# Placing side jobs' stages by the clock of their first engine in a four-layer gated cross-attention kernel

## The chip, the cores and the metric

The kernel runs on one core of a Trainium2 chip. The metric is the device time of one execution in microseconds (us). Engines are named as in the profile: PE (TensorE matmul), PEld (its weight loads), DVE (VectorE), ACT (ScalarE), POOL (GpSimd), SP (SyncE, which here only issues DMAs). Names such as L222 are lines of the kernel before the change.

## The reference, cut to what matters

Sixteen sequences of 128 tokens with 256 features (`x`), a context of the same shape, and four layers. Each layer adds a gated cross-attention and a gated feed-forward part to `x`:

```python
for l in range(4):
    x = x + tanh(g_xattn[l]) * xattn[l](layernorm(x), ctx)
    x = x + tanh(g_ffn[l]) * ffn[l](layernorm(x))
```

The attentions of layers 0 to 2 have 16 heads of 16 features; layer 1 takes its softmax over the queries and layer 2 has a mask on keys. Layer 3 has 8 heads of 64 features, and its keys and values come from the normalized context together with the normalized `x`. The feed-forward parts of layers 0, 2 and 3 are mixtures of 8 experts of which each token uses the best two; layer 2 has a shared expert besides. Layer 1 is a linear layer with a gated low-rank addition (LoRA). Everything is float32.

```python
probs, idx = top_k(softmax(h @ w_gate.T), 2)
y = sum(probs[j] * expert[idx[j]](h) for j in range(2))
```

## The kernel before, in words

**Tiling.** A sequence is one tile of 128 tokens; four sequences make a block, so there are 16 sequences in 4 blocks. `xs[b]` stays in SBUF throughout. PSUM has eight banks in two pools of four: `ps_mm` (attention scores, experts' hidden values) and `ps_x` (all else). Code that doesn't assume small score ranges (`layers(fast=False)`) is there for other inputs and is not run here.

**Attention.** `attend` runs an attention as a software pipeline over sequences. Step n does `scores` of sequence n (values projection `ps_v`, 16 score matmuls into the four `ps_mm` banks, four exps on ACT), `values` of sequence n-1 (`ps_o`, in layers 0 and 2 with row sums by a matmul and a reciprocal on DVE), and `output` of sequence n-2 (`ps_y`, then the addition to `x` on DVE, L348). Layers 1 and 2 run in one call, as 32 steps.

**Side jobs.** What else the attention needs is written as Python generators, one per block: `queries` (layer norm, transposes, projection, L1165 on), `keys`, the routing of a block that is done (`Moe.front`), and for layer 1 `Lora.run`. A layer norm takes statistics on DVE, `ve` on DVE (L217 or L219), a logarithm and an exponential on ACT (L222, L224), three DVE operations (L227 to L230), and four activations per block on ACT (L306). `front` computes the router's logits, a softmax, the best two experts, the place of every row, and scatters the rows to `xg` in DRAM with eight indirect DMAs on POOL (L529). After some blocks `plan` (L598 on) works out on DVE which expert each slot of 128 rows belongs to; SP reads its result into registers. A generator yields where another engine's result is needed. `yield Pe(...)` says that the next stage begins with matmuls; a plain number says that it doesn't; zero says that it may start at once.

**What sets the order.** PE, ACT and DVE execute in the order in which Python issues instructions (`manual_schedule`, L1483); the other queues, SP and POOL among them, are ordered by the framework. `Clock` (L1311) is a model of the engines' times: `note` adds up each issued instruction's estimated cost and keeps when each tile is written and read. `now()` is PE's time in it. `run_stage` runs one stage of a job and notes the time at which its results are ready. `poll` runs stages that aren't `Pe` as long as any is ready by `now()`; `whole` polls and then runs one ready `Pe` stage; `idle` does the same or moves the PE clock on; `tick` spends up to `share` us of PE time on such work between the parts of a step; `tick.until(tiles)` idles until tiles are ready. The model's waits of an instruction are for its inputs, its engine and the tiles that it overwrites by name, not for a PSUM bank that is used anew under another name.

**Layer 0's early experts.** Once block 1 is routed, a plan gives nine slots that are surely full. `start` (L2352) makes a generator for them, and runs its first stage at once: it issues the loads of rows (L759) and weights (L1533) on SP. `early` (L2356) is the filler: `attend` takes it up when all scores are issued, and interleaves its stages with the routing of blocks 2 and 3. The other 30 slots follow after `attend`. In layers 1 and 2 the filler is the shared expert, in layer 3 the slots (`open_end`).

Of the kernel before, what the change touches and what calls it, by code (L numbers as in the profile page):

```python
# [90 lines left out]
def kernel(ctx: ExitStack, tc: tile.TileContext, a: dict, out: bass.AP):  # L91
    nc = tc.nc
# [4 lines left out]
    rpool = ctx.enter_context(tc.tile_pool(name="route", bufs=2))  # L97
    xtpool = ctx.enter_context(tc.tile_pool(name="xnT", bufs=NBLK))
    dram = ctx.enter_context(tc.tile_pool(name="rows", bufs=1, space=DRAM))
    ps_mm = ctx.enter_context(tc.tile_pool(name="ps_mm", bufs=4, space=PSUM))  # L100
    ps_x = ctx.enter_context(tc.tile_pool(name="ps_x", bufs=4, space=PSUM))

# [96 lines left out]
    class Pe(int):  # L199
        pass  # L200

    def finish(job):

        while True:
            try:
                next(job)
            except StopIteration as end:
                return end.value


    def inverse_sd(var, n, twice):

        ve = stat.tile([P, n], F32, tag="ve", name="ve")
        if twice:
            nc.vector.tensor_scalar(ve, var, 1.0 + 1e-5, 1e-10, ALU.mult, ALU.add)  # L217
        else:
            nc.vector.tensor_scalar(ve, var, 1e-5, None, ALU.add)  # L219

        lv = stat.tile([P, n], F32, tag="sd", name="lv")
        nc.scalar.activation(lv, ve, AF.Ln)  # L222
        r0 = stat.tile([P, n], F32, tag="r0", name="r0")
        nc.scalar.activation(r0, lv, AF.Exp, scale=-0.5)  # L224
# [71 lines left out]
    def normalized(srcs, mv, rstd):  # L296

        nmr = stat.tile([P, len(srcs)], F32, tag="nmr", name="nmr")
        nc.vector.scalar_tensor_tensor(nmr, mv[:, :, 0], -1.0, rstd, ALU.mult, ALU.mult)  # L299
        yield 1  # L300
        while len(held) > 2 and held[-3] is not None:
            yield 1
        xns = stat.tile([P, len(srcs), ROW], F32, tag="xn", name="xn", bufs=3)
        held.append(xns)
        for i, src in enumerate(srcs):
            nc.scalar.activation(  # L306
                xns[:, i, 0:D], src, AF.Identity, bias=nmr[:, i:i + 1], scale=rstd[:, i:i + 1]
            )
            if i == 1:
                yield 1  # L310
        return xns
# [48 lines left out]
    def softmax8(lg):  # L360
# [3 lines left out]
        nc.vector.tensor_tensor(d, lg, bc(m), ALU.subtract)  # L364
        yield 1
        e = small("sm_e")
# [55 lines left out]
    class Moe:  # L422
# [14 lines left out]
        def front(self, blk, plan=None, bias=None):  # L437
# [8 lines left out]
            next(soft)  # L446
            yield 1
            next(soft)
            if self.layer == 2:
                yield 2  # L450
# [654 lines left out]
    class Fast16:  # L1105
# [86 lines left out]
        def scores(self, b, tick):  # L1192
# [17 lines left out]
            else:  # L1210
                nc.vector.tensor_copy(v, pv)

# [96 lines left out]
    }  # L1309

    class Clock:  # L1311

# [18 lines left out]
        def cost(self, ins, out, srcs):  # L1331
# [16 lines left out]
            if ins.engine == mybir.EngineType.Activation:  # L1348
                return 0.13 + n * 0.7e-3 + (0.04 if len(srcs) > 2 else 0.0)
            if ins.engine == mybir.EngineType.Pool:  # L1350
                return 0.1 + n * 2.6e-3
            if kind == "InstReciprocal":
                return 0.1 + n * 6.5e-3
            return 0.07 + n * 0.97e-3

# [21 lines left out]
        def when(self, *tiles):  # L1377
            return max(self.done.get(t.tensor.name, 0.0) for t in tiles)

    def attend(parts, filler=None, open_end=False, hurry=True, share=2.5):  # L1380

# [5 lines left out]

        clock = Clock()
        jobs, filling, waiting = [], [], []

# [3 lines left out]
        def run_stage(job):  # L1394
            clock.ends, clock.moved = [], []
            try:
# [8 lines left out]
                return  # L1405
            job[2] = isinstance(n, Pe)
            ends = clock.ends or clock.moved
# [5 lines left out]
        def poll():  # L1413
            while True:
                for job in list(jobs):
                    if not job[2] and job[1] <= now():
                        run_stage(job)
                        break
                else:
                    return  # L1420

        def whole():
            poll()
            for job in jobs:
                if job[2] and job[1] <= now() + 0.1:
                    run_stage(job)
                    return True
            return False

        def idle(limit):  # L1430


            if whole():
                return
            times = [job[1] for job in jobs] + [limit]
            if filling and min(times) > now() + 0.3:
                if filling[0][1] <= now() + 0.1:
# [5 lines left out]
        class Tick:  # L1443
# [12 lines left out]
            def urgent(self):  # L1456
                for job in jobs:
                    if job[3] and job[2] and job[1] <= now() + 0.1:
                        run_stage(job)
                        self.urgent()  # L1460
                        return
# [7 lines left out]

        def begin(gen, pe, key=False):  # L1470
            return [gen, max(now(), clock.at[mybir.EngineType.DVE]) if not pe else 0.0, pe, key]

        def ahead(att, before, blk):
            made = att.prepare(blk, before(blk) if before is not None else None)
            made = [begin(job, False) for job in made]
            jobs.extend(made)
# [6 lines left out]
        with tc.manual_schedule(engines=IN_ORDER):  # L1483
            ln_exp()
            prepared = ahead(*blocks[0][:2], 0)
            for n in range(len(steps) + 2):
                tick.left = share
                if n == len(steps) - 1 and open_end:
                    next(filler)
                if n == len(steps) and filler is not None:  # L1490
                    filling.append(begin(filler, True))
                if n < len(steps):
# [7 lines left out]
                    tick()  # L1500
                    att, b = steps[n]
                    att.scores(b, tick)
                if 1 <= n <= len(steps):
                    tick.urgent()
                    att, b = steps[n - 1]
                    att.values(b, tick)
                if n >= 2:
                    att, b = steps[n - 2]
                    att.output(b, tick)
                    if b % BPB == BPB - 1:  # L1510
                        _, _, behind, blk = blocks[(n - 2) // BPB]
                        job = begin(behind(blk), False, hurry)
                        waiting.append(job)
# [736 lines left out]
    def layers(fast):  # L2250
# [40 lines left out]
        with tc.tile_pool(name="context", bufs=1) as cpool, ExitStack() as for_mid:  # L2291
# [16 lines left out]
            with tc.tile_pool(name="att0", bufs=2) as pool:  # L2308
# [43 lines left out]
                def start(plan):  # L2352
                    started.append(slots0(moe, n, [plan], lanes, tiles(fpool, bufs0)))
                    next(started[0])

                def early():  # L2356
                    while not started:
                        yield Pe(1)
                    yield from started[0]
# [7 lines left out]
                if fast:  # L2367
                    att = Fast16(0, pool, keys_in(pool), w, ctxT, watch)
                    attend([(att, clear, behind)], early())
                else:  # L2370
# [235 lines left out]
```

## Time and profile before

| what | value |
|---|---|
| time, median of 3 runs | 1597.12 us (1596.69 to 1597.88) |
| the profiled execution | 1658.12 us |
| its span, first to last instruction | 1656.4 us |
| mean granted PE clock in it | 0.959 |
| instructions | 34906 |

The profiled execution is longer than the other runs; times read from its trace are its own. The work lies in it like this:

| from to (us) | what |
|---|---|
| 0 to 22.7 | loads, first block's queries and keys |
| 22.7 to 145.0 | attention 0 with routing of blocks 0 and 1 |
| 145.0 to 156.4 | from there to the first expert slot |
| 156.4 to 437 | layer 0's expert slots |
| 437 to 719 | attentions 1 and 2 with LoRA and routing |
| 719 to 870 | layer 2's shared expert |
| 870 to 1204 | layer 2's expert slots |
| 1204 to 1480 | contexts, attention 3 |
| 1480 to 1627 | layer 3's expert slots |
| 1627 to 1656.4 | gathering and storing of the result |

In rows of the timeline the columns are start, duration, engine, line, operation, tiles (written <- read), and the number of instructions merged into the row; in brackets stands how long the engine sat idle before it, and what ended that. In rows of waits they are engine, tile and line, what it waited for, total us, times, longest us. "issue" and "remote" stand for no cause that the profile sees.

### The profile page before, as it was taken

The page shows a single profiled execution, that of the slowest core. Times are in us where ns is not written, and L with a number is a line of the kernel's source. Part 1 is how long each engine was busy: PE and PEld are TensorE (multiplying, and loading weights), DVE is VectorE, ACT ScalarE, POOL GpSimd, SP SyncE. Part 2 cuts the span into 40 slices and gives each one's busy share as a digit, 9 for nine tenths or more (in the row PEclk, how much of TensorE's full clock was granted, in tenths as well). Part 3 has the DMA queues.
Part 4 walks back from the last instruction along what each step waited for, and adds up shares of the span by engine and source line. Part 5 has one row for each costly group of instructions (what it writes and reads, how often), then busy time and mean ns, then how long its engine had stood idle before and what let it go on. Part 6 is the DMA issues. An engine that isn't in the chain of part 4 may idle for free.

```text
span 1656.4 us, 34906 instructions
## 1 busy us (share of the span) xinstructions
PE 1510.9 (91%) x12752; PEld 1189.5 (72%) x12752; DVE 878.1 (53%) x2835; ACT 634.4 (38%) x1526; POOL 365.5 (22%) x470
## 2 busy tenths in 40 slices
PE   6984989999998999899999999999999998977892
PEld 4763889999755667555559999999846665667792
DVE  4775312222267866676445555556734554566554
ACT  4643423335455556553225333334443323231110
POOL 4222411111442122433000111011150002023331
PEclk9997999999999999999999999999999999998896
DMA  9604575525330000111065413310260000033856
GB/s 333 236 28 161 188 243 168 167 66 173 86 48 1 2 2 27 41 40 52 1 207 162 148 46 134 122 34 28 97 121 2 14 2 27 2 103 126 267 182 206
DMA packets 107769, 169.30 MB, mean 102 GB/s; under 512 B 17081, under 2 KB 77950, under 8 KB 107584
## 3 DMA queue, kind: packets, MB, share of 16 engines
q1 hardware_dynamic: 83744, 111.99, 21.3%
q0 software_dynamic: 20304, 49.66, 9.6%
q10 hardware_dynamic: 3536, 5.25, 0.9%
q8 instruction: 108, 1.77, 0.4%
q14 instruction: 77, 0.63, 0.1%
HBM read 268.42 MB, written 48.18 MB: 191 GB/s over the span
## 4 chain that ended last, share of the span: by engine, by line


## 5 line engine op out<-in xcount | busy, mean ns | idle before, releaser
L1757 PEld LDWEIGHTS ps_w<-xT,w 128*128 128x128 f32 x2304 | 264.2, 192 | 2.5 <-issue 0.2
L1757 PE MATMUL ps_w<-xT,w 128*128 128x128 f32 x2304 | 265.0, 275 | 0.0
L841 POOL DMA_INDIRECT yd<-y,to x117 | 118.1, 1010 | 578.9 <-DVE c L804 304.9
L829 PE MATMUL ps_e<-w,hT 128*128 128x256 f32 x848 | 197.6, 380 | 2.0 <-DVE hT L1664 1.6
L829 PEld LDWEIGHTS ps_e<-w,hT 128*128 128x128 f32 x848 | 154.5, 190 | 21.0 <-DVE hT L1664 2.6
L1765 ACT ACTIVATE u<-ps_w,b 128x128 f32<-128x128 f32 x312 | 89.3, 367 | 175.9 <-PE ps_w L1757 161.8
L1580 PE MATMUL ps_h<-xT,w 128*128 128x128 f32 x1120 | 139.5, 285 | 13.2 <-DMA w<-in_l_w_dram 7.3
L1580 PEld LDWEIGHTS ps_h<-xT,w 128*128 128x128 f32 x1120 | 137.5, 201 | 16.4 <-issue 9.3
L1768 DVE SCALAR_TENSOR_TENSOR m<-ps_w,b,u 128x128 f32<-128x128 f32 x312 | 87.7, 345 | 111.3 <-PE ps_w L1757 90.6
L1585 ACT ACTIVATE hT<-ps_h,b 128x128 f32<-128x128 f32 x312 | 88.9, 372 | 127.1 <-issue 83.7
L529 POOL DMA_INDIRECT xg<-xn,xi x96 | 93.4, 973 | 108.2 <-issue 41.7
L1694 PE MATMUL ps_w<-xnT,sw 128*128 128x512 f32 x256 | 111.9, 593 | 0.0
L837 DVE SCALAR_TENSOR_TENSOR y<-ps_e,c,bias 128x256 f32<-128x256 f32 x78 | 37.6, 483 | 129.0 <-PE ps_e L829 128.0
L1087 POOL TENSOR_TENSOR sum_range<-sum_range,rs 128x256 f32<-128x256 f32 x48 | 35.3, 735 | 284.2 <-DVE rs L2174 146.0
L1694 PEld LDWEIGHTS ps_w<-xnT,sw 128*128 128x128 f32 x256 | 48.2, 190 | 56.4 <-issue 51.1
L794 DVE COPY xT<-ps_xr 128x256 f32<-128x256 f32 x117 | 48.6, 418 | 73.1 <-PE ps_xr L792 66.7
L1235 ACT ACTIVATE e<-ps_s 128x512 f32<-128x512 f32 x128 | 65.9, 602 | 43.9 <-PE ps_s L1220 33.9
L1287 DVE RECIPROCAL rs<-ps_o 128x256 f32<-128x256 f32 x32 | 56.2, 1755 | 49.7 <-PE ps_o L1276 30.2
L306 ACT ACTIVATE xn<-x,nmr,rstd 128x256 f32<-128x256 f32 x128 | 68.3, 598 | 30.9 <-DVE nmr L299 19.3
L1220 PE MATMUL ps_s<-qM,kT 32*128 32x256 f32 x768 | 62.3, 411 | 6.5 <-ACT e L1235 5.4
L1276 PE MATMUL ps_o<-e,v 128*32 128x128 f32 x1536 | 55.7, 287 | 13.4 <-ACT logitsT L412 5.3
L821 ACT ACTIVATE bias<-b,c 128x256 f32<-128x256 f32 x78 | 40.4, 518 | 62.6 <-DVE c L807 18.8
(273 smaller groups left out, 2562.6 us busy)
## 6 DMA issues: line engine op xcount, KB each, us to landing
w<-in_l_w_dram SPq DMA_DIRECT2D x156, 1024.0 KB
w<-in_l_w_dram SPq DMA_DIRECT2D x39, 512.0 KB
kT<-in_l_wgu_dram SPq DMA_DIRECT2D x39, 512.0 KB
xg<-zeros POOLq DMA_DIRECT2D x15, 1170.0 KB
xr<-xg SPq DMA_DIRECT2D x78, 130.0 KB
b<-in_l_b_dram SPq DMA_DIRECT2D x78, 128.0 KB
kT<-in_l_w_dram SPq DMA_DIRECT2D x39, 256.0 KB
x<-yd POOLq DMA_DIRECT2D x48, 128.0 KB
```

The source lines that it names most:

```text
L306: nc.scalar.activation(xns[:, i, 0:D], src, AF.Identity, bias=nmr[:, i:i + 1], scale=rstd[:, i:i + 1])
L529: self.unordered(nc.gpsimd.indirect_dma_start(out=xg[:, :], in_=xns[:, i, :], in_offset=None, out_offset=bass.IndirectOffsetOnAxis(ap=xi[: ...
L829: nc.tensor.matmul(po, lhsT=hT[:, f, :], rhs=lane(s)["w2"][:, f, :], start=(f == 0), stop=(f == nf - 1),)
L841: self.unordered(nc.gpsimd.indirect_dma_start(out=yd[:, :], in_=y, in_offset=None, out_offset=bass.IndirectOffsetOnAxis(ap=to[:, 0:1], axi ...
L1220: nc.tensor.matmul(pss[j][:, 2 * c:2 * c + 2, :], lhsT=self.kT[blk][part, c, tok], rhs=self.qM[blk][part, c, :, tok], start=True, stop=True,)
L1235: nc.scalar.activation(e, pss[j], AF.Exp)
L1580: nc.tensor.matmul(ps[:, i, :], lhsT=w["w1"][:, k, f * P:(f + 1) * P], rhs=xT[:, k, :], start=(k == 0), stop=(k == KC - 1),)
L1585: nc.scalar.activation(hT[:, f, :], ps[:, i, :], AF.Gelu, bias=w["b1"][:, f:f + 1])
L1694: nc.tensor.matmul(ps, lhsT=wt[:, k, f * P:(f + 1) * P], rhs=xnT[:, k, :], start=(k == 0), stop=(k == KC - 1),)
L1757: nc.tensor.matmul(ps[:, f, :], lhsT=wt[:, k, s, f * P:(f + 1) * P], rhs=xT[:, k, :], start=(k == 0), stop=(k == KC - 1),)
L1765: nc.scalar.activation(u[:, f, :], pair[0][:, f, :], AF.Identity, bias=w["b1"][:, i:i + 1])
L1768: nc.vector.scalar_tensor_tensor(m1[:, f, :], pair[1][:, f, :], w["b3"][:, i:i + 1], u[:, f, :], ALU.add, ALU.mult,)
```

## The change

- A second mark besides `Pe`, `Act`, tells that a stage begins on ACT. It is put at the yields ahead of the exps, the normalizing activations and, as a new yield, the logarithm of `inverse_sd`. A plain number now means DVE.
- `poll` makes one pass over all jobs and the filler. A stage that isn't `Pe` is run if it is ready by PE's time or by its first engine's own time + 0.15 us, whichever is later.
- A `Pe` stage is run only when the `ps_x` bank that the next tile gets is free too: `Ring` keeps the tiles made, and `bank()` is the time at which the fourth last was last read.
- Scores of a sequence are issued after the exps of the sequence before have ended by the clock (`tick.until(*last)`).
- Layer 0's early slots are in `filling` from the start (`eager`), waiting with plain yields until a plan is there; so `poll` issues their first loads, in place of `start`. Their `Pe` stages still wait until all scores are issued.
- Layer 0's copy of the values projection goes from DVE to ACT (L1211).
- The clock's cost of ACT and DVE instructions with more operands goes up, and a new job's ready time no longer counts DVE's clock.

```diff
+    class Act(int):
+        pass
+
@@ inverse_sd
+        yield Act(1)
         lv = stat.tile([P, n], F32, tag="sd", name="lv")
         nc.scalar.activation(lv, ve, AF.Ln)
@@ normalized
-        yield 1
+        yield Act(1)
         while len(held) > 2 and held[-3] is not None:
-            yield 1
+            yield Act(1)
...
             if i == 1:
-                yield 1
+                yield Act(0)
@@ Fast16.scores, layer 0
-                nc.vector.tensor_copy(v, pv)
+                nc.scalar.copy(v, pv)
@@ Clock.cost
-                return 0.13 + n * 0.7e-3 + (0.04 if len(srcs) > 2 else 0.0)
+                return 0.13 + n * 0.7e-3 + (0.15 if len(srcs) > 2 and n > 64 else 0.0)
...
-            return 0.07 + n * 0.97e-3
+            return 0.07 + n * 0.97e-3 + (0.1 if n > 64 and len(srcs) > 1 else 0.0)
@@ attend
-            job[2] = isinstance(n, Pe)
+            job[2] = type(n)
...
         def poll():
-            while True:
-                for job in list(jobs):
-                    if not job[2] and job[1] <= now():
-                        run_stage(job)
-                        break
-                else:
-                    return
+            for job in jobs + filling:
+                if job[2] is not Pe and job[1] <= max(
+                    now(), clock.at[DVE if job[2] is int else ACT] + 0.15
+                ):
+                    run_stage(job)
...
-                if job[2] and job[1] <= now() + 0.1:
+                if job[2] is Pe and max(job[1], bank()) <= now() + 0.1:
...
-            times = [job[1] for job in jobs] + [limit]
-            if filling and min(times) > now() + 0.3:
+            times = [max(job[1], bank()) if job[2] is Pe else job[1] for job in jobs]
+            times.append(limit)
+            if filling and filling[0][2] is Pe and n >= len(steps) and min(times) > now() + 0.3:
...
+        def bank():
+            return max((clock.read.get(t.tensor.name, 0.0) for t in ps_x.made[-4:-3]), default=0.0)
+
-        def begin(gen, pe, key=False):
-            return [gen, max(now(), clock.at[mybir.EngineType.DVE]) if not pe else 0.0, pe, key]
+        def begin(gen, kind, key=False):
+            return [gen, 0.0 if kind is Pe else now(), kind, key]
...
+            if eager:
+                filling.append(begin(filler, int))
+            last = []
...
+                    tick.until(*last)
                     att.scores(b, tick)
+                    last = att.es[b]
@@ layer 0's early slots
                 def start(plan):
                     started.append(slots0(moe, n, [plan], lanes, tiles(fpool, bufs0)))
-                    next(started[0])
 
                 def early():
                     while not started:
-                        yield Pe(1)
+                        yield 1
                     yield from started[0]
...
-                    attend([(att, clear, behind)], early())
+                    attend([(att, clear, behind)], early(), eager=True)
```

More of the change, by code (lines that the diff above doesn't have):

```diff
@@ L98, with __init__, tile @@
     xtpool = ctx.enter_context(tc.tile_pool(name="xnT", bufs=NBLK))
+    class Ring:
+        def __init__(self, pool):
+            self.pool, self.made = pool, []
+        def tile(self, *args, **kwargs):
+            t = self.pool.tile(*args, **kwargs)
+            self.made.append(t)
+            return t
     dram = ctx.enter_context(tc.tile_pool(name="rows", bufs=1, space=DRAM))
     ps_mm = ctx.enter_context(tc.tile_pool(name="ps_mm", bufs=4, space=PSUM))
-    ps_x = ctx.enter_context(tc.tile_pool(name="ps_x", bufs=4, space=PSUM))
+    ps_x = Ring(ctx.enter_context(tc.tile_pool(name="ps_x", bufs=4, space=PSUM)))
     xs = []
@@ L364, in softmax8 @@
         nc.vector.tensor_tensor(d, lg, bc(m), ALU.subtract)
-        yield 1
+        yield Act(1)
         e = small("sm_e")
@@ L446, in front @@
             next(soft)
-            yield 1
+            yield Act(1)
             next(soft)
             if self.layer == 2:
-                yield 2
+                yield 1
                 p = finish(soft)
@@ L1309 @@
     }
+    DVE, ACT = mybir.EngineType.DVE, mybir.EngineType.Activation
     class Clock:
@@ L1377, in when, with attend @@
         def when(self, *tiles):
-            return max(self.done.get(t.tensor.name, 0.0) for t in tiles)
-    def attend(parts, filler=None, open_end=False, hurry=True, share=2.5):
+            return max((self.done.get(t.tensor.name, 0.0) for t in tiles), default=0.0)
+    def attend(parts, filler=None, open_end=False, hurry=True, share=2.5, eager=False):
         clock = Clock()
+        n = 0
         jobs, filling, waiting = [], [], []
@@ L1457, in urgent @@
                 for job in jobs:
-                    if job[3] and job[2] and job[1] <= now() + 0.1:
+                    if job[3] and job[2] is Pe and max(job[1], bank()) <= now() + 0.1:
                         run_stage(job)
@@ L1468, in attend @@
         tick = Tick()
-        def begin(gen, pe, key=False):
-            return [gen, max(now(), clock.at[mybir.EngineType.DVE]) if not pe else 0.0, pe, key]
+        def bank():
+            return max((clock.read.get(t.tensor.name, 0.0) for t in ps_x.made[-4:-3]), default=0.0)
+        def begin(gen, kind, key=False):
+            return [gen, 0.0 if kind is Pe else now(), kind, key]
         def ahead(att, before, blk):
             made = att.prepare(blk, before(blk) if before is not None else None)
-            made = [begin(job, False) for job in made]
+            made = [begin(job, int) for job in made]
             jobs.extend(made)
@@ L1489, in attend @@
                     next(filler)
-                if n == len(steps) and filler is not None:
-                    filling.append(begin(filler, True))
+                if n == len(steps) and filler is not None and not eager:
+                    filling.append(begin(filler, Pe))
                 if n < len(steps):
@@ L1511, in attend @@
                         _, _, behind, blk = blocks[(n - 2) // BPB]
-                        job = begin(behind(blk), False, hurry)
+                        job = begin(behind(blk), int, hurry)
                         waiting.append(job)
@@ L2353, in start @@
                     started.append(slots0(moe, n, [plan], lanes, tiles(fpool, bufs0)))
-                    next(started[0])
                 def early():
                     while not started:
-                        yield Pe(1)
+                        yield 1
                     yield from started[0]
```

## The prediction

> **What bounds the kernel now.** First the page's busy time, then its split by stage, then the waits inside the stages that the change touches.
>
> ```profile
> PE 1510.9 (91%) x12752; PEld 1189.5 (72%) x12752; DVE 878.1 (53%) x2835; ACT 634.4 (38%) x1526; POOL 365.5 (22%) x470
> ```
>
> TensorE (PE) is the bound on average, so only time in which PE stands still is to be won, and only in the stretches ordered by `attend`. The view of engine busy time by stretch (columns: stretch, length, busy time of PE, PEld, DVE, ACT, POOL, granted clock, DMA share, GB/s) cuts the span there:
>
> ```profile
> 22.70:145.00 122.30, 103.41 (x1534) 75.48 (x1533) 83.69 (x231) 62.13 (x129) 35.88 (x44) 0.92 0.41 157
> 145.00:156.40 11.40, 0.78 (x4) 0.34 (x3) 7.82 (x50) 1.92 (x4) 0.15 (x1) 0.50 0.75 228
> 156.40:437.00 280.60, 269.86 (x1798) 252.40 (x1799) 66.82 (x297) 113.32 (x362) 53.81 (x55) 0.97 0.50 162
> 437.00:719.00 282.00, 258.29 (x2766) 172.13 (x2765) 198.49 (x526) 155.29 (x307) 89.78 (x126) 0.96 0.14 30
> 1204.00:1480.00 276.00, 264.63 (x2635) 168.78 (x2635) 136.17 (x360) 88.85 (x183) 49.49 (x60) 0.98 0.16 37
> ```
>
> These are attention 0, the junction to its experts, the experts of layer 0, attentions 1 and 2, attention 3. PE idles 122.3 - 103.4 = 18.9, 10.6, 10.7, 23.7 and 11.4 us. The experts' slots are PE's own time and get the same instructions; they only begin earlier or later. The densest idle time is the junction, 10.6 of 11.4 us. Its timeline:
>
> ```profile
> 139.20 0.61 DVE L639 TENSOR_TENSOR past<-iota,end 128x72 f32<-128x72 f32 x1
> ...
> 144.90 0.48 DVE L348 SCALAR_TENSOR_TENSOR x<-ps_y,gate,x 128x256 f32<-128x256 f32 x1 [5.09 <-PE ps_y L1298]
> ...
> 146.06 0.22 DVE L645 TENSOR_REDUCE eid<-past 128x9 f32<-128x72 f32 x1
> ...
> 148.87 0.18 DVE L675 CAST plan_i<-plan 128x36 int32<-128x36 f32 x1
> ...
> 149.83 0.37 SPq L759 DMA_DIRECT2D xr<-xg  x1
> ```
>
> The plan of the early slots (L608 to L677) starts at 132.8 us and its second stage ends at 139.8. The next one, from L645, needs nothing more, but stands behind L348 in DVE's queue, which waits for PE. So the plan is whole at 149.1 and the first rows are asked for at 149.8, after attention 0 has ended (PE's last router transpose ends at 145.1). SP's queue, asked what it waited for between 120 and 160 us, shows a second lock:
>
> ```profile
> SPq L926 <- DVE x L348: 78.8, 1, 78.8
> ```
>
> The loads of the next layers' attention weights (L926) stand ahead of the first slot's loads and wait 78.8 us for attention 0's memory. Last, what PE waited for, from 22.7 to 157 us and from 437 to 719 us:
>
> ```profile
> PE ps_xr L792 <- DMA xr<-xg: 7.8, 1, 7.8
> ...
> PE ps_h L1580 <- DVE cw L483: 2.9, 1, 2.9
> ...
> PE ps_s L1220 <- ACT e L1235: 2.1, 1, 2.1
> ```
> ```profile
> PE ps_ln L329 <- ACT xn L306: 5.5, 3, 4.1
> PE ps_o L1276 <- ACT logitsT L412: 5.3, 1, 5.3
> PE ps_s L1220 <- ACT e L1235: 3.3, 1, 3.3
> ```
>
> 7.8 + 2.9 is the junction. The 4.1 us at 511 us is a block border: L227 on DVE could run at 509.7 (its input r ends then) but runs at 513.7, behind four sums. The 5.3 us at 690 us falls into a row of scatters on POOL (L529, 683.5 to 693.6), in which ACT and DVE start nothing for 11.1 and 3.1 us; that is not a matter of order, and I leave it.
>
> [...] ACT stood 73.9 us in 24 waits of L222 for L219. [...] for a 1024 KB weight; the trace has 151.16 to 156.36, 5.2 us, which I use.
>
> **The change, part by part** (us of the profiled execution).
>
> *Poll rule, `Act` marks, `eager`, at the junction.* A stage that begins on DVE is placed once its input is ready by DVE's own clock, not PE's. A stage that follows a DVE stage of its own job is therefore due at the next poll: its ready time is that stage's end + 0.1, and DVE's clock + 0.15 is no less. So L645 to L677 (3.0 us on DVE, 146.06 to 149.13, other work between) come soon after L639, ahead of L348: plan at about 143 even if nothing before it moves. One poll runs at most one stage per job, but a step has some ten polls. Block 1's routing (L219 at 89.1 to L526 at 129.0, 40 us for some 20 stages) shortens too. The scatters (8 x (0.97 + 0.30) = 10.2 us on POOL) move with it, past POOL's sums (L1087, 0.73 each), which nothing waits for. What is late next: these scatters, ending at 139.6 unmoved; then rows 3.0 us (149.83 to 152.83) and weights about 5.2 us, so PE starts by 147; with scatters 5 us earlier, at 145. Gain 8.5 to 10.6, and up to 2.8 more where the second slot waited for weights at 163.0. This holds if SP's order turns, so that row loads come ahead of L926; SP's order isn't written by `attend`, but L926 can't go before 145 and the rows then can, so I expect it. If not, the loads go at about 148.3, gain 1.5. I take 9. `eager` itself only moves the first loads from the planning stage to the same or next poll: nothing, since 0.5 us of model time is far inside the wait for scatters; without that cover, 0.5.
>
> *The same rules in the rest of attention 0.* Gaps of PE over 0.4 us that DVE, ACT or PSUM ended: 2.1 at 24.5, where exps stood behind L222, and 0.5 + 0.6 + 0.6 + 0.7 + 1.1 + 1.1 + 0.6 + 0.6 = 5.8. I take 3 of 7.9; range 0 to 7.
>
> *Copy v on ScalarE.* 16 x 402 ns = 6.4 us leave DVE (83.7 to 77.3 of 122.3), 16 x 384 ns (L1284, the same shape) = 6.1 join ACT (62.1 to 68.2). Neither bounds the stretch, so nothing by itself: PE's side jobs and scores cover it. Queued behind the copy are four exps, which wait for later matmuls anyway. Without the cover, 0.4 per step lost, or as much won where DVE is late: -3 to +3.
>
> *Attentions 1 and 2.* The block border 3 of 4.1; the 3.3 us at 467, 1; of the small waits for DVE (about 6.5 in all) a third. I take 6; range 0 to 10.
>
> *Attention 3.* 3.9 us at 1459.7 lie in scatters again: 0. Of 2.8 + 1.2 + 2.5 us at 1480 to 1491, where slots wait for DVE behind routing, 1; range -3 to 4, since routing stages that now queue sooner can stand before a slot's copy.
>
> *Waits added.* Scores wait for the four exps of the sequence before (2.06 us of ACT), side jobs for one of four banks. Hardware waits for those banks anyway; queued behind the scores on PE are the values of the sequence before, which need the same exps. Cost where the model is late: 0 to 5, I take 2. ACT's queue now gets normalizations (L306) ahead of exps: 0 to 31 (below), I take 3. The new cost constants only shift the clock and lie within these.
>
> Sum: 9 + 3 + 6 + 1 - 2 - 3 = 14 us of 1658.1 (span 1656.4 and 1.7 around it). The runs' median, 1597.1, is 61.0 us below this execution; scaled by 1597.1/1658.1 = 0.963 that is 13.5, so 1583.6 us.
>
> **Rivals.** *SP keeps its order* (or the change doesn't do there what it says). For it: L926 stands first today though it comes much later in the program. Against: today it is also ready earlier than the rows. The junction then gives 1.5, the sum is 6.5, times 0.963 is 6.3: 1590.8.
>
> *Slower: normalizations before exps.* The attentions run 34 layer norms (12 for queries, 8 routing, 4 LoRA, 10 in layer 3), each with four activations of 605 ns, 2.4 us. If each goes ahead of four exps and PE has no side job to fill in, PE loses what exceeds ACT's slack; at 0.9 us each that is 31. Against the gains of 19 it is 12 more, times 0.963: 1608.7. It decides from 19/34 = 0.56 us each. For it: exps end PE's waits already twice (2.1 and 3.3). Against: ACT is busy only 51 to 55% there.
>
> *Gaps move elsewhere*: PE's slots at 0.5 clock after a pause, weights late instead of rows, small waits reforming: 1597.
>
> **How the numbers follow.** Forecast 0.60 (1570 to 1593), SP's order 0.16, slower 0.20, moved 0.04. Beyond 0.2% (3.2 us), about what a measurement of this kernel tells from none: faster 0.59 + 0.11 = 0.70; slower 0.20; same 0.10. The range leaves out the best tenth of the forecast and half of the slower case: 1571 to 1607.
>
> **What would show it.** Right: L645 follows L639 within 1 us; row loads (L759) stand before L926 on SP; the gap before the first L1580 is under 3 us; L222's waits fall well under 73.9 us; L227 at the border of layer 1 precedes the sums. Wrong: PE's waits for exps in `ps_s` and `ps_o` grow past 19 us; L926 stays first; or the first slot waits for weights as long as it waited for rows.

## The result, and the profile after

The change makes the kernel slower: 1620.9 us (1617.8 to 1622.7) against 1597.5 us, ratio 1.014 with a 95% interval of 1.012 to 1.016. The forecast was 1583.6 us and faster. On another chip the ratio was 1.0085 (1.006 to 1.011): the sign holds, and the loss is smaller there.

The profiled execution of after took 1622.7 us, its span is 1620.9 us. Lines of code lie 14 or 15 further down than in the kernel before up to L1300, and 25 further from L1580 on: L219 is L233, L926 is L941, L794 is L809, L1580 is L1605, L1805 is L1830. The page's busy line:

```profile
PE 1493.9 (92%) x12752; PEld 1178.0 (73%) x12752; DVE 872.5 (54%) x2819; ACT 652.0 (40%) x1552; POOL 366.2 (23%) x470
```

The trace that the prediction was worked from is of an execution of 1658 us. The kernel before was therefore profiled once more (first experiment), with a span of 1596.9 us; that trace is the base of all comparisons below. Its busy line:

```profile
PE 1486.3 (93%) x12752; PEld 1172.4 (73%) x12752; DVE 877.9 (55%) x2835; ACT 633.4 (40%) x1526; POOL 365.6 (23%) x470
```

Here is its busy time by stretch (stretch, length, busy time and instructions of PE, PEld, DVE, ACT, POOL, granted clock, DMA share, GB/s), cut where the work changes: attention 0, the junction after it, layer 0's slots, attentions 1 and 2, the shared expert, attention 3, layer 3's slots and the end (layer 2's slots are left out):

```profile
22.70:129.80 107.10, 98.00 (x1538) 72.61 (x1536) 82.78 (x229) 62.02 (x129) 32.62 (x40) 0.97 0.46 176
129.80:144.30 14.50, 0.69 (x2) 0.30 (x3) 8.84 (x50) 1.92 (x4) 3.55 (x5) 0.55 0.71 212
144.30:417.80 273.50, 263.97 (x1783) 247.10 (x1784) 66.69 (x298) 110.58 (x357) 52.82 (x54) 0.97 0.51 165
417.80:691.60 273.80, 256.82 (x2782) 171.68 (x2781) 198.74 (x527) 157.71 (x312) 90.78 (x127) 0.98 0.14 31
691.60:842.20 150.60, 146.18 (x455) 78.76 (x453) 80.32 (x232) 47.91 (x75) 29.66 (x34) 1.00 0.23 79
1216.70:1443.60 226.90, 222.13 (x2546) 149.10 (x2545) 126.78 (x348) 74.29 (x156) 28.09 (x36) 1.00 0.08 26
1443.60:1596.90 153.30, 116.39 (x852) 108.95 (x852) 95.63 (x423) 20.77 (x48) 53.47 (x55) 0.89 0.65 212
```

And the kernel after, cut at the same pieces of work:

```profile
22.70:128.20 105.50, 93.97 (x1507) 71.15 (x1505) 77.87 (x226) 63.72 (x138) 35.10 (x43) 0.95 0.48 183
128.20:135.20 7.00, 0.41 (x2) 0.22 (x3) 3.11 (x7) 0.00 (x0) 1.11 (x2) 0.74 0.54 178
135.20:418.20 283.00, 270.66 (x1816) 251.89 (x1817) 73.19 (x328) 123.08 (x374) 52.86 (x55) 0.97 0.51 165
418.20:691.60 273.40, 256.10 (x2713) 170.21 (x2712) 198.43 (x536) 158.10 (x311) 91.58 (x128) 0.98 0.14 30
691.60:849.70 158.10, 152.52 (x523) 83.25 (x521) 80.18 (x222) 48.38 (x76) 29.44 (x34) 0.98 0.22 76
1225.80:1459.20 233.40, 220.30 (x2538) 148.13 (x2537) 130.79 (x371) 72.65 (x153) 29.87 (x37) 0.99 0.08 26
1459.20:1620.90 161.70, 119.03 (x860) 109.79 (x860) 91.52 (x398) 27.61 (x55) 51.88 (x55) 0.90 0.62 200
```

Read the lengths in pairs. The junction falls from 14.5 to 7.0 us: PE's first slot starts at 135.2 instead of 144.3, 9 us earlier, as forecast. Layer 0's slots then take 9.5 us longer, and reach their last group of matmuls at 418.2 instead of 417.8. More than half of both numbers is a change of order: 33 of PE's matmuls (attention 0's last output projections, and some of a block's norm and router), 5.1 us in all, run ahead of the first slot in the kernel before and behind it in after (the slots' stretch has 1816 matmuls instead of 1783). So what is won ahead of the slot is some 4 us. It is lost again behind it, as 2.8 us more of idle time of PE (9.5 before, 12.3 after) and some 1.6 us of slower matmuls. The first shared expert's matmul comes at the same time in both kernels, but after has more of attention 2 left then (523 PE instructions in the stretch, not 455). From there on it only loses. The last scores of attention 2 make a fairer cut there; with it the whole difference reads (us, differences in brackets):

| from, to | before | after | capped at 1 us (below) |
|---|---|---|---|
| start to first early slot | 144.3 | 135.2 (-9.1) | 142.0 (-2.3) |
| layer 0's slots | 273.5 | 283.0 (+9.5) | 274.1 (+0.6) |
| attentions 1 and 2, to the last scores | 266.9 | 270.8 (+3.9) | 261.3 (-5.6) |
| to layer 2's first slot | 157.5 | 160.8 (+3.3) | 155.2 (-2.3) |
| layer 2's slots, contexts | 374.5 | 376.0 (+1.5) | 376.0 (+1.5) |
| attention 3, to layer 3's first slot | 226.9 | 233.4 (+6.5) | 226.3 (-0.6) |
| layer 3's slots and the end | 153.3 | 161.7 (+8.4) | 153.3 (0.0) |
| span | 1596.9 | 1620.9 (+24.0) | 1588.2 (-8.7) |

**The longest pause: layer 3's first slot.** PE's timeline of after around it (start, length, line, tiles; in brackets the idle time before and its releaser):

```profile
1449.42 0.44 PE L807 MATMUL ps_xr<-ident,qT 128*128 128x128 f32 x2 [0.41 <-DVE rs L2199]
1459.23 2.08 PE L1830 MATMUL ps_g<-xT,kT 128*128 128x128 f32 x8 [9.37 <-DVE xT L809]
```

The rows are transposed at 1449.9, and PE then waits 9.4 us for a copy of 0.4 us (L809). DVE's timeline of the same kernel says what it did instead:

```profile
1451.14 0.15 DVE L385 TENSOR_REDUCE sm_s<-sm_e 128x4 f32<-128x32 f32 x1
...
1458.62 0.22 DVE L665 TENSOR_REDUCE ahead<-past 128x8 f32<-128x64 f32 x1
1458.76 0.41 DVE L809 COPY xT<-ps_xr 128x256 f32<-128x256 f32 x1
```

From 1451.1 to 1458.8 DVE works without a pause through the routing and the plan of a block, from its softmax (L385) to the plan's third stage (L665). The copy stands behind all of it. In the kernel before the same copy, L794, stands ahead of the next routing stage (L488):

```profile
1443.18 0.42 DVE L794 COPY xT<-ps_xr 128x256 f32<-128x256 f32 x1
...
1447.88 0.15 DVE L488 TENSOR_TENSOR ns<-cw 128x4 f32<-128x4 f32 x1
```

**The same thing at the junction.** DVE in after, near the end of attention 0: the plan (its stages at L654 and L690) is whole at 119.8 us, where the base has it at 135.3, and stands ahead of the reciprocal (L1302) that attention 0 needs. PE has written what this reciprocal reads by 113.2, but from 113.0 to 120.2 DVE goes through routing and plan (L385 to L700) without a pause:

```profile
117.80 0.23 DVE L654 TENSOR_TENSOR past<-iota,end 128x72 f32<-128x72 f32 x1
...
119.66 0.18 DVE L690 CAST plan_i<-plan 128x36 int32<-128x36 f32 x1
...
120.19 1.75 DVE L1302 RECIPROCAL rs<-ps_o 128x256 f32<-128x256 f32 x1
121.98 0.42 DVE L1304 TENSOR_TENSOR oT<-ps_o,rs 128x256 f32<-128x256 f32 x1
```

PE in after, in the same stretch and behind it:

```profile
122.55 2.05 PE L1313 MATMUL ps_y<-w_att,oT 128*128 128x256 f32 x4 [4.86 <-DVE oT L1304]
...
135.22 3.61 PE L1605 MATMUL ps_h<-xT,w 128*128 128x128 f32 x16 [3.71 <-DMA w<-in_l_w_dram]
...
150.74 1.12 PE L422 MATMUL ps_logitsT<-xnT,wgl 128*32 128x128 f32 x16 [2.92 <-ACT xnT L348]
```

PE, which has other work until then, stops for 4.9 us at 117.7, which the kernel before doesn't do. The slot then begins early, but its first matmuls wait 3.7 us for weights with the last output projections of attention 0 behind them in PE's queue (they run at 138.7), and ACT's queue stood 19.9 us at a slot's bias (L836, behind its DMA). At 150.7 PE waits for ACT again, which loaded tables between the early slots' gelu and the routing's logarithm and exponential:

```profile
147.20 1.28 ACT L237 ACT_TABLE_LOAD   x1
148.49 0.20 ACT L237 ACTIVATE lv<-ve 128x4 f32<-128x4 f32 x1
```

From 130 to 236 us after has ten such loads, the kernel before four.

**A short wait, and a lower clock behind it.** By the shared expert, where layer 2's routing goes on, PE in after reads:

```profile
718.76 3.60 PE L1719 MATMUL ps_w<-xnT,sw 128*128 128x512 f32 x8
724.50 0.41 PE L487 MATMUL ps_rank<-both,tri 128*128 128x32 f32 x2 [2.15 <-DVE both L482]
...
727.79 6.00 PE L1719 MATMUL ps_w<-xnT,sw 128*128 128x512 f32 x8
```

The wait is 2.15 us; the same eight matmuls then take 6.00 us instead of 3.60. The granted clock is 1.00 from 716 to 722.3 us, 0.71 from 722.3 to 734, and 0.62 in the stretch of the slower eight (727.8 to 734); in the base it is 1.00 in every slice of 10 us from 690 to 760. Not each such pause is followed by a lower clock: after 2.94 us from 1465.2 it is 1.00 to 1473, and after 2.39 us from 1508.8 it is 1.00 to 1523. What decides it isn't in the traces. Of the 24 us, 16.4 are idle time of PE (1596.9 - 1486.3 = 110.6 before, 1620.9 - 1493.9 = 127.0 after), and 7.6 are the same 12,752 matmuls taking longer.

### The profile page after: what moved, and what is told of

It reads as the page before. It is cut to its first block, busy times and chain, and to the rows that moved or that the text cites. A ratio compares the mean times of both kernels' runs of the same rounds, so it can differ in the third digit from the quotient of the medians.

```text
span 1620.9 us, 34904 instructions
## 1 busy us (share of the span) xinstructions
PE 1493.9 (92%) x12752; PEld 1178.0 (73%) x12752; DVE 872.5 (54%) x2819; ACT 652.0 (40%) x1552; POOL 366.2 (23%) x470
## 4 chain that ended last, share of the span: by engine, by line
## 5 line engine op out<-in xcount | busy, mean ns | idle before, releaser
L1605 PE MATMUL ps_h<-xT,w 128*128 128x128 f32 x1120 | 139.1, 285 | 11.7 <-DMA w<-in_l_w_dram 10.9
L1605 PEld LDWEIGHTS ps_h<-xT,w 128*128 128x128 f32 x1120 | 137.1, 201 | 14.8 <-issue 11.7
L809 DVE COPY xT<-ps_xr 128x256 f32<-128x256 f32 x117 | 48.6, 418 | 66.1 <-PE ps_xr L807 66.1
L1302 DVE RECIPROCAL rs<-ps_o 128x256 f32<-128x256 f32 x32 | 56.1, 1753 | 34.3 <-PE ps_o L1291 27.1
L1250 ACT ACTIVATE e<-ps_s 128x512 f32<-128x512 f32 x128 | 65.9, 604 | 17.9 <-PE ps_s L1235 17.9
L836 ACT ACTIVATE bias<-b,c 128x256 f32<-128x256 f32 x78 | 40.3, 516 | 79.8 <-DMA b<-in_l_b_dram 36.2
L2178 ACT ACTIVATE e<-ps_s 128x512 f32<-128x512 f32 x64 | 33.3, 600 | 81.4 <-PE ps_s L2172 81.4
```

Source lines behind the costliest of these rows:

```text
L1250: nc.scalar.activation(e, pss[j], AF.Exp)
L1302: nc.vector.reciprocal(rs, po[:, 1])
L1605: nc.tensor.matmul(ps[:, i, :], lhsT=w["w1"][:, k, f * P:(f + 1) * P], rhs=xT[:, k, :], start=(k == 0), stop=(k == KC - 1),)
```

## The experiments

Theory A, formed on these lines: the new poll places a stage when its input is ready by its own engine's clock. A stage that follows a DVE stage of its own job always is, so each poll adds one more stage of the chain to DVE's queue, whatever the time on PE. DVE's queue runs ahead, and the next copy or reciprocal that PE needs is placed behind several us of routing. Theory B: the added waits (scores after exps, banks) and the copy of v on ACT cost it. Kernels of one group ran on one chip beside the kernel before.

**The kernel before, once more.** No edit.

> The kernel before, unchanged. Its shown profile has a span of 1656.4 us, while its timed runs take 1596.7 to 1601.4; the kernel after takes 1620.9 in its profile and 1617.8 to 1622.7 in its runs. Theory A (the shown profile of before is one disturbed execution): the new profile has a span of about 1595 to 1600 us, and 60 us of pauses of the shown one are gone, mostly while rows are being scattered. Theory B (the profiler itself slows this kernel): the new profile is again near 1656 us. The timed ratio is 1.000 within 0.3% in both.

Measured: 1598.2 us, ratio 0.9995 (0.998 to 1.001), profiled span 1596.9. Profiling doesn't slow this kernel: the profiled run took 1598.7 us, among runs of 1593.6 to 1603.3. "A disturbed execution" was not the whole answer either, as later groups showed: on two other chips every run of the kernel before took 1655 to 1667 us. The trace behind the prediction is like those; see the last section.

**First group: which part.** The capped rule limits how far a stage may be placed ahead of PE:

```diff
-                if job[2] is not Pe and job[1] <= max(
-                    now(), clock.at[DVE if job[2] is int else ACT] + 0.15
-                ):
+                own = clock.at[DVE if job[2] is int else ACT] + 0.15
+                if job[2] is not Pe and job[1] <= max(now(), min(own, now() + 1.0)):
```

> The kernel after, with one line more in the poll rule: a DVE or ACT stage may still be placed by its engine's own clock, but at most 1.0 us ahead of PE's. Theory A (run-ahead): in the kernel after each poll places one more stage of a routing chain whatever PE's time is, so up to 7.6 us of routing and planning stand on DVE ahead of a copy that PE waits for (4.9 us at the end of attention 0, 9.4 us before layer 3's first slot); with the cap most of the 23 us come back: 1594 to 1604 us, and no pause of PE over 4 us between 1430 and 1520 us. Theory B (the added waits: scores after the exps, side jobs when a bank is free, the copy of v on ACT): the cap changes nothing of those, 1614 to 1624 us.

Measured: 1584.8 us, ratio 0.9926 (0.991 to 0.994), and the table's last column. This is below both kernels, and 9 us below what theory A allowed; PE's pauses from 1430 to 1520 us stay under 4 us (3.4), as it said.

The old poll, with all else as after except the early slots' start:

```diff
-            for job in jobs + filling:
-                if job[2] is not Pe and job[1] <= max(
-                    now(), clock.at[DVE if job[2] is int else ACT] + 0.15
-                ):
-                    run_stage(job)
+            while True:
+                for job in list(jobs):
+                    if job[2] is not Pe and job[1] <= now():
+                        run_stage(job)
+                        break
+                else:
+                    return
```

> The kernel after with the old poll (a stage that isn't Pe is placed when it is ready by PE's clock, as long as any is) and the old start of layer 0's early slots; marks, bank rule, scores after the exps, copy of v on ACT and the new costs stay. Theory A (run-ahead of DVE's queue): 1594 to 1604 us, the loss is gone and so is the win at the junction. Theory B (the added waits): 1614 to 1624 us.

Measured: 1600.4 us, ratio 1.0024 (1.000 to 1.004).

The opposite: of the whole change only the marks and the new `poll`. Undone in after:

```diff
-                nc.scalar.copy(v, pv)
+                nc.vector.tensor_copy(v, pv)
...
-            for job in jobs + filling:
+            for job in list(jobs):
...
-                if job[2] is Pe and max(job[1], bank()) <= now() + 0.1:
+                if job[2] is Pe and job[1] <= now() + 0.1:
...
-                    tick.until(*last)
...
-                    attend([(att, clear, behind)], early(), eager=True)
+                    attend([(att, clear, behind)], early())
```

(and the old costs, `start`, `begin` and the old conditions in `idle` and `urgent`).

> The kernel before with the new poll rule and its marks alone: no bank rule, no scores after the exps, v copied on DVE, the old costs, the old start of the early slots. Theory A (run-ahead): 1610 to 1626 us, with a pause of PE of more than 5 us before layer 3's first slot. Theory B (the added waits): 1592 to 1602 us.

Measured: 1622.1 us, ratio 1.018 (1.015 to 1.021). PE's waits from 1400 to 1560 us in this kernel (line, what it waited for, total, times, longest) begin with

```profile
PE ps_g L1826 <- DVE xT L809: 13.1, 2, 9.6
```

The same 9.4 to 9.6 us as in after. These three runs settle between A and B: the rule alone makes the whole loss, without it the rest costs 0.2%, and a limit on it turns the loss into a gain. In the capped kernel the same view from 1400 to 1530 us begins with

```profile
PE ps_g L1829 <- DVE xT L809: 6.1, 3, 3.4
```

The cap keeps the single pass over the jobs and limits only how early a stage is placed. It does so for DVE's stages and for ACT's at once, and no run limits one alone; but PE's waits, added up over the span by the engine that ended them, point at DVE: 27.7 us in the base, 48.5 in after, 48.0 with the rule alone and 32.1 with the cap. Those that ACT ended are 16.1, 17.6, 11.4 and 10.5 us.

The rule in attention 0 alone:

```diff
-                    now(), clock.at[DVE if job[2] is int else ACT] + 0.15
+                    now(), clock.at[DVE if job[2] is int else ACT] + 0.15 if eager else 0.0
```

> The kernel after with the new poll rule in attention 0 alone; in attentions 1 to 3 a stage waits for PE's clock again (one stage of a job per poll). All else as after. Theory A (run-ahead, and the 9 us won at the junction are given back before the slots of the second plan at 226 us): the losses of 7.6 us by the shared expert and 14 us in layer 3 go, the junction's start stays early, and the time is 1594 to 1603 us, no better than before. Rival C (the win at the junction is real to the end and only layers 2 and 3 hide it): 1585 to 1591 us. Theory B (the added waits): 1612 to 1624 us.

Measured: 1605.1 us, ratio 1.006 (1.004 to 1.009), 2 us above what A allowed. Its first early slot starts at 135.4 us, and layer 0's slots reach their last group at 419.1: 8.9 us earlier and 10.2 longer, nearly the numbers of after, with the same 1816 matmuls behind the slot's start. So nothing of the junction's start outlives layer 0, and the later layers don't hide a win; rival C falls. Of the 10.9 us that its span is above the base, 4.9 lie in layer 2's slots and contexts (379.4 against 374.5 us), where the rule doesn't act; I have no cause for them.

**Second group: how far, and is it the clock?** This chip runs the kernel before in 1660.5 us, so ratios are compared. The edit, against the capped kernel:

```diff
-                if job[2] is not Pe and job[1] <= max(now(), min(own, now() + 1.0)):
+                if job[2] is not Pe and job[1] <= max(now(), min(own, now() + 4.0)):
```

> The kernel after with its stages placed at most 4.0 us ahead of PE's clock, in place of 1.0. Theory A (what costs is how far a side job's chain runs ahead of PE on DVE): the time lies between those of the cap of 1.0 and of none, 1592 to 1612 us, and the pause before layer 3's first slot is between 2.4 us and 9.4 us. Rival D (any cap does, since it only breaks the endless chain): 1582 to 1588 us.

Measured: 1673.0 us, ratio 1.0081 (1.006 to 1.010); the pause before layer 3's first slot is 4.9 us:

```profile
PE ps_g L1829 <- DVE xT L809: 9.1, 2, 4.9
```

The pause is between the 2.4 us with the cap of 1 us and the 9.4 without, as A has it; in time 4 us are as bad as no limit (1.0085 on a chip with the same time of the kernel before). Rival D falls: what matters is how far the chain runs ahead.

The clock takes ACT's table loads for nothing. After, uncapped, with a clock that adds them (34 in its trace):

```diff
+            self.funcs = (AF.Ln, AF.Exp)
...
+                func = getattr(ins, "func", AF.Copy)
+                if func not in (AF.Copy, AF.Identity, *self.funcs):
+                    self.funcs = (func,)
+                    each += 1.28
...
+            if isinstance(ins, mybir.InstLoadActFuncSet):
+                self.funcs = (AF.Ln, AF.Exp)
+                self.at[mybir.EngineType.Activation] += 1.28
```

> The kernel after, uncapped, but its clock adds 1.28 us for every table that ACT has to load (the trace has 35 of these loads, which the clock takes for nothing). Theory E (the rule is right and only the clock is wrong: with the loads known, stages and slots fall where they can run): 1583 to 1600 us, with under 3 us of pause before layer 3's first slot. Theory A (run-ahead does not depend on that error): 1610 to 1628 us, and that pause stays over 6 us.

Measured: 1667.0 us, ratio 1.0036 (1.002 to 1.005), between the two theories. Its pause at layer 3's first slot is unchanged; its view of PE's waits from 1490 to 1600 us begins with

```profile
PE ps_g L1839 <- DVE c L819: 9.4, 1, 9.4
```

The same clock in the capped kernel:

> The kernel with the cap of 1.0 us, and the clock that knows the loads of ACT's tables. If those loads are a second cost of their own (10 in layer 0's early slots in the kernel after, 4 before): 1574 to 1582 us. If the cap already does what there is to do: 1582 to 1588 us. If the new clock only shuffles the work: anywhere from 1580 to 1600 us, and no stage with a plain reason.

Measured: 1649.5 us, ratio 0.9929 (0.991 to 0.995), the same as the cap alone on a chip of the faster kind (0.9926). As far as two chips can be compared, the loads are no second lever once the chains don't run ahead.

The capped rule alone on the kernel before (the edit of the rule-only kernel, with the cap):

> The kernel before with the poll rule capped at 1.0 us and its marks, and nothing else of the change: no bank rule, no scores after the exps, v copied on DVE, old costs, old start of the early slots. If the gain of the capped kernel is the rule's own: 1582 to 1590 us. If it needs the other parts too (banks, exps, costs), which the old poll with them does not show by itself (1600): 1592 to 1600 us.

Measured: 1662.3 us, ratio 1.0009 (1.000 to 1.002). The capped rule without the other parts gains nothing, as the second case has it; what the other parts add was asked in the last two groups.

**Third and fourth group: one part less.**

The kernel after, without an edit:

> The kernel after, unchanged, on the same chip as the three runs beside it, since chips differ (1595 to 1598 us for the kernel before on two of them, 1660 on a third). Theory A (run-ahead is a matter of order, so the loss shows on every chip): ratio to before 1.010 to 1.018.

Measured: 1673.7 us, ratio 1.0085 (1.006 to 1.011). The loss is there, but it is smaller than the 1.010 to 1.018 that was expected.

The kernel after with the clock that knows the table loads, as in the second group:

> The kernel after with the clock that knows the loads of ACT's tables, uncapped, now beside the kernel after on one chip. If the unknown loads carry most of the loss (as 1.0036 on the slower chip lets one think): 0.990 to 1.005 of before and over 0.9% faster than after. If the run-ahead carries it whatever the clock knows: at least 1.007 of before, within 0.7% of after.

Measured: 1670.9 us, ratio 1.0064 (1.005 to 1.008), beside after's 1.0085 on the same chip: within 0.7% of after as the second case has it, though 0.06% below its bound of 1.007. On this one chip the loads are 0.2 of the 0.85%, with overlapping intervals, and not most of the loss. The first run of this kernel, 1.0036 on another chip, would make them 0.5%; that the same kernel differs by 0.3% between two chips also says how little differences of this size mean across chips.

The capped kernel without the wait for exps:

```diff
-                    tick.until(*last)
```

> The kernel with the cap of 1.0 us, without the wait of the scores for the exps of the sequence before. The prediction put 0 to 5 us on that wait. If it costs, as predicted: 2 us below the capped kernel, ratio to before 0.989 to 0.993. If it is the part that the cap needs (the cap on the kernel before, without exps, banks and costs, came to 1.0009): 0.996 to 1.003.

Measured: 1649.1 us, ratio 0.9931 (0.991 to 0.995). This group has no capped kernel with the wait; against 0.9926 and 0.9929 on other chips no effect of the wait can be told, and the 2 us that the prediction gave it (0.1%) are too few for these runs.

The capped kernel with every bank taken as free:

```diff
         def bank():
-            return max((clock.read.get(t.tensor.name, 0.0) for t in ps_x.made[-4:-3]), default=0.0)
+            return 0.0
```

> The kernel with the cap of 1.0 us, without the rule that a side job's matmuls wait for a free bank of PSUM. The prediction put it at next to nothing, since the hardware waits for that bank anyway: ratio 0.991 to 0.995. If it is the part that the cap needs, because without it PE stands at a bank with other work behind: 0.996 to 1.003.

Measured: 1651.8 us, ratio 0.9952 (0.994 to 0.997), 0.2% above the run beside it; the intervals overlap. It lies just outside the first case (0.991 to 0.995), and below the second. That PE waits for a bank also where the poll has no such rule is in the trace of the kernel before, from 22.7 to 157 us:

```profile
PE ps_ln L329 <- DVE qM L1181: 1.3, 2, 1.1
```

DVE writes nothing that these transposes read; L1181 reads `ps_q`, another tile of `ps_x`.

The capped kernel with v on DVE and the old costs (first kernel), with v on DVE alone (second), and with the old start of the early slots (third, the edit shown last):

```diff
-                nc.scalar.copy(v, pv)
+                nc.vector.tensor_copy(v, pv)
...
-                return 0.13 + n * 0.7e-3 + (0.15 if len(srcs) > 2 and n > 64 else 0.0)
+                return 0.13 + n * 0.7e-3 + (0.04 if len(srcs) > 2 else 0.0)
...
-            return 0.07 + n * 0.97e-3 + (0.1 if n > 64 and len(srcs) > 1 else 0.0)
+            return 0.07 + n * 0.97e-3
```
```diff
+                    next(started[0])
...
-                        yield 1
+                        yield Pe(1)
...
-                    attend([(att, clear, behind)], early(), eager=True)
+                    attend([(att, clear, behind)], early())
```

> The kernel with the cap of 1.0 us, with the clock's old costs of ACT and DVE instructions and v copied on DVE again. The prediction said that the new costs lie within the other terms and the copy within 3 us. If so: ratio to before 0.990 to 0.996. If the truer clock is what the capped rule needs (its stages are placed by it, and the capped rule without this came to 1.0009): 0.997 to 1.003, with the loss by the shared expert, after 690 us.

> The kernel with the cap of 1.0 us, v copied on DVE in layer 0, the new costs kept. If the costs are what matters in the run beside it: 0.990 to 0.996, as the capped kernel. If the copy is: 0.997 to 1.003.

> The kernel with the cap of 1.0 us, with the old start of layer 0's early slots (first loads issued by the plan, PE's stages as filler after all scores). The prediction put this part at nothing. If so: 0.990 to 0.996. If the early slots in the queue of side jobs from the start are what the capped kernel gains by: 0.997 to 1.003.

Measured: 1591.8 us, 0.9960 (0.995 to 0.997); 1586.7 us, 0.9933 (0.991 to 0.995); 1586.3 us, 0.9917 (0.989 to 0.995). The copy and the start make no difference that these runs can tell. The costs are worth some 0.3% (0.9960 against 0.9933), again with intervals that overlap; 0.9960 is at the upper bound of what the prediction's case allowed. If they add up, banks and costs (0.2 and 0.3%) are somewhat over half of the 0.8% between the capped rule alone and the capped change, which ran on different chips; the rest isn't attributed.

## Why the prediction was wrong

**The failed step** is the price of the poll rule: 19 us of gain (9 + 3 + 6 + 1) were booked for it and what comes with it, and the rule alone made the kernel 1.8% slower. The prediction saw the mechanism: "A stage that follows a DVE stage of its own job is therefore due at the next poll". It booked that as gain alone, asked what waits for the moved stages, and not what they were moved ahead of. On DVE those are the attention's reciprocals and copies and the slots' copies, all of which PE waits for. The nearest it came is attention 3, "routing stages that now queue sooner can stand before a slot's copy", at up to 3 us; it cost 6.5 us before the first slot and 8.4 behind it (pauses of 2.9, 3.4, 1.5 and 2.4 us up to 1511 us, ended by DVE, ACT, DVE and a load of weights, against 2.1 and 2.9 before; what each of them costs wasn't tried).

**The junction.** Its mechanism was right in most of its signs: L660 (L645 before) follows L654 by 0.3 us; the rows are asked for at 128.9, ahead of L941, which goes at 282; the first slot starts 9.1 us earlier (9 was taken). That the numbers agree is in part luck, since 5.1 of the 9.1 us are work that now stands behind the slot. One sign failed: PE's gap right before the first L1605 is 3.7 us, where under 3 were given, as the weights are what is late. The plan came 15.4 us earlier, however (about 6 was expected), and delayed attention 0 by a pause of 4.9 us; the rows gain only 8.0 of that, since SP waits 8.0 us for the scatters, which are what is late next. And "the experts' slots are PE's own time and get the same instructions; they only begin earlier or later" failed: layer 0's slots became 9.5 us longer, by the 33 matmuls that moved behind the first slot, and by the waits and the slower matmuls shown above (2.8 and some 1.6 us; the granted clock is 0.97 over both stretches). What is due to which wait wasn't tried singly. The run with the rule in attention 0 alone shows that nothing of the earlier start outlives layer 0.

**Attentions 1 and 2.** 6 us of gain were taken; after loses 3.9 by the last scores. The waits named do shrink: those of L237 (L222) for L233 (L219) fall from 73.2 to 20.8 us. At the block border L242 (L227) still doesn't precede the sums: its input is ready at 480.4 us, and it runs at 484.1, behind four of them, so this sign failed. PE's wait there is 1.0 us instead of 4.1 all the same; one of the border's two norms now begins 11 us earlier (L233 at 479.7 us, L219 at 490.6 in the base). With the cap the stretch is 5.6 us shorter, near the 6 that were taken, and with the capped rule alone it is still 3.7 shorter than in the trace of the prediction (274.7 against 278.4 us, both of the slower kind of chip). So the gain was there, and the run-ahead ate it.

**The rest.** The copy of v was put at nothing, and no run tells it from nothing. The wait for exps was put at -2 us, which the runs can't tell from nothing either. The bank rule, held for a cost at most, may gain 0.2%, and the clock's costs, held to lie within other terms, 0.3%; both are at the edge of what these runs tell. The slower rival had the right sign (1608.7 us, 0.20) and the wrong mechanism: PE waits for exps 0.9 us in attention 0 and 1.0 in attentions 1 and 2 in after, less than before (1.4 and 2.2), while normalizations ahead of exps were to cost 31 us. The slower rival should have been the general one, of stages placed early on an engine's queue ahead of work that PE waits for: on DVE 7.6 us of routing and plan (1451.1 to 1458.8) stood ahead of L809, and PE waited 9.4 us. The last rival's slots at half clock are in the trace that it was made from: behind the junction's pause the first 16 matmuls of the first slot take 3.76 us at a granted clock of 0.50 (156.4 to 160.0 us), and the next 16 take 2.03 us at 1.00 (160.4 to 162.4). After has the same pair, 3.61 us at 0.54 (135.2 to 138.8) and 2.02 us at 1.00 (145.8 to 147.8).

**The base.** The trace behind the prediction had 60 us that these runs don't have, so its gaps (2.9 us before the first L1580, 3.9 us at 1459.7) were partly another chip's. Also the lock that it wanted to open at the junction is small in the base: there L645 (131.2 us) follows L639 (129.9) by 1.3 us, and the loads of L926 are out of the way 0.9 us after the plan is whole. That changed sizes, not the sign: after is slower on both kinds of chip.

## What to carry to other kernels

When a list scheduler may place work by the clock of a side engine, limit how far it may run ahead of the engine that bounds the kernel: here a limit of 1 us turned +1.4% into -0.7%, and one of 4 us left the loss as it was (1.008 and 1.0085 on two chips of one kind). The limited rule gained only together with the change's other parts; alone it came to 1.001. For every step that is moved earlier in an engine's queue, list what it now stands ahead of and who waits for that, before counting what it frees. And profile the base more than once: compare the trace's own time with the other runs first.

## What the runs showed of the hardware

The kernel before took 1595 to 1598 us in three groups, on two chips, and 1660 in two groups on two other chips: 4% more. In the slower trace the extra time sits mostly in stretches with rows of indirect scatters on POOL. Matched row by row, it falls 8 to 9 us further behind from the start of each of six of the twelve rows (at 102, 684, 1373, 1452, 1498 and 1525 us) to the next row or the end, and not at all behind the three by the shared expert (728 to 785). DVE at the same two instructions of the same kernel, on a chip of the slower kind (the trace of the prediction):

```profile
1454.22 0.17 DVE L630 TENSOR_SCALAR skip<-cnt 128x8 f32<-128x8 f32 x1
1460.64 0.69 DVE L2184 TENSOR_TENSOR oT<-ps_o,rs 128x512 f32<-128x512 f32 x1 [6.24 <-PE ps_v L2126]
```

and in the trace of 1596.9 us:

```profile
1419.93 0.17 DVE L630 TENSOR_SCALAR skip<-cnt 128x8 f32<-128x8 f32 x1
1420.01 0.68 DVE L2184 TENSOR_TENSOR oT<-ps_o,rs 128x512 f32<-128x512 f32 x1
```

The releaser named, ps_v, isn't what L2184 reads; ACT stands still for 9.2 us (1453.8 to 1463.0) at the same row of scatters. The twelve rows of scatters themselves take 9.8 to 10.0 us each in both traces. What holds the engines isn't in the traces.
